# Copies moved behind exponentials and tails moved into the next softmax, in a one-core cross-attention kernel

## The chip, the cores and the metric

The kernel runs on one core of one Trainium2 chip. The metric is the device time of one execution in microseconds; for the kernel before it is the median of three runs. One more execution was profiled, and all lines quoted come from that one.

A core has five engines that run side by side, each with its own queue of instructions, in the order in which the program issues them. The profile calls them PE (matrix products, with PEld for its weight loads), DVE (VectorE), ACT (ScalarE), POOL (GpSimd) and SP (here it only issues DMAs). They wait for each other through semaphores.

## The reference

Layer norm, a query projection, attention over 32 heads of width 32 with keys and values taken straight from a context, an output projection, and the residual. Eight batches, 256 queries, 256 keys, width 1024, all float32.

```python
x = (hidden_states - mu) * rsqrt(var + LN_EPS) * ln_gamma + ln_beta
Q = split_heads(x @ Wq.T)
K = split_heads(memory_keys)                  # the same context for both
V = split_heads(memory_values)
scores = einsum('bhsd,bhtd->bhst', Q, K) * HEAD_DIM ** (-0.5)
scores = where(mask, scores, -inf)
probs = softmax(scores, axis=-1)
attn = einsum('bhst,bhtd->bhsd', probs, V)
out = attn.transpose(0, 2, 1, 3).reshape(B, S, HIDDEN) @ Wout.T
return residual + out
```

## The kernel before

**Quads.** The work is cut into 64 quads: four heads of one batch, eight quads to a batch (`N = 64`, `NQ = 8`). One loop over n walks through them as a software pipeline. Loop n issues, for PE in this order: the scores of quad n+1 (L471), some steps of an output product (L675), the values of quad n-2 (L605), more steps, a query projection (L332) or a query product (L432), and more steps. `softmax(n + 1)` is issued within the same loop, behind values n-2; it works on the scores just made, mostly on DVE, ACT and POOL.

**One softmax.** For each of the four heads j and both halves s of the queries, `exps(j)` issues a DVE pass that reads the scores in PSUM, adds the mask and finds a minimum (L505), and an ACT exponential that also sums (L509). `normalize(j)` is a DVE reciprocal (L516) and two POOL scalings (L518). `blocks(j)` transposes 32 by 32 blocks on DVE into the tile pT (L524). `aside(0)` and `aside(1)` copy half of pT for two heads each to the tile pc on ACT (L530). The last transpose `blocks(3)`, `aside(1)` and four DMAs on SP (pT to pT, L585, and pc to pT, L589), with the loop's loads and sends between them (`between`), form a function `tail`. After it pT has the layout that values need. For quads 0 to 7 the tail is put on a list `tails` and run within the next softmax, behind `exps(0)`; for all later quads it runs at once.

**Where the copies stand.** Behind `exps(0)` and the tails, `softmax_parts` copies finished values from PSUM to SBUF on ACT (`copy_at`, L618, two copies for a quad). The values have one pair of PSUM tiles, so the next values wait for these copies.

**Output products.** The output projection of a batch is done by seven products of 512 columns (`PRODUCTS`, four steps each, every step two matmul instructions in the profile), while the next batch's quads run. Their sums and differences of blocks are made on POOL (`sum_at`, L658). They accumulate in one PSUM bank (`ps_o`, one buffer). For batches 0 to 5 the first product, A11, is issued in loops n = 9, 17, 25, 33, 41 and 49 between scores and values; `keep_p1` (L683, ACT) then copies the bank, and the second product, A12, accumulates further into the same bank: three steps later in the same loop, the fourth in the next. `keep_p1` reaches the softmax as the hook "p1", run behind `exps(0)`. Later takes and stores from the bank are DVE instructions (L713, L717), hooked into later softmaxes. The same hooks mechanism isn't used for batch 6: its products (`ENDS`, one a loop, n = 56 to 62) run while the last batch's quads do, and their copies out of the bank (`keep_p1` at n = 57, `take_po_q`, L696, at n = 58, `copy_po`, L693, at n = 59 to 63) are issued ahead of the softmax of the loop. POOL adds them to the residual (`add_kept`, L701), SP sends them (L704). From n = 59 on, two matmul instructions a loop also go to the last batch's own output (L725).

**Query sums.** For batches 3 to 7 the query projection works on sums of blocks of the normalized input, made on POOL (`sum_x`, L422) from a tile that DMAs on SP fill (`move_x`, L319).

**Buffers.** e: 4; pT, pc: 3; scores: 4 PSUM banks, one for each head; values: one pair of tiles; `po`: one bank.

Of the kernel before, what the change touches and what calls it, by code (L numbers as in the profile page):

```python
# [59 lines left out]
def xattn_kernel(  # L60
# [16 lines left out]
    NQ = NC  # L77
# [9 lines left out]
    N = B * NQ  # L87
# [368 lines left out]
    mbs, scs, pTs, pvs, ats, pos = {}, {}, {}, {}, {}, {}  # L456
# [19 lines left out]
    def softmax(*args):  # L476
        for _ in softmax_parts(*args):
            pass

    tails = []  # L480

    def softmax_parts(n, copies=(), between=(), hooks={}, fill=()):

        fill = list(fill)

        def fill_in():
            if fill:  # L490
                fill.pop(0)()

        pss = scs[n]
        pT = pTs[n] = ptp.tile([P, 2, NI, NH, NS, K], F32, tag="pT", name=f"pT_{n}")
        pc = asp.tile([P, NI, NH, NS, K], F32, tag="pc", name=f"pc_{n}")
        es, mns, dens = {}, {}, {}

        def exps(j, part=range(NS)):
            if 0 in part:
                es[j] = ep.tile([P, NS, T], F32, tag="e", name=f"e_{n}_{j}")  # L500
                mns[j] = sm.tile([P, NS], F32, tag="mn", name=f"mn_{n}_{j}")
                dens[j] = sm.tile([P, NS], F32, tag="den", name=f"den_{n}_{j}")
            e, mn, den = es[j], mns[j], dens[j]
            for s in part:
                nc.vector.tensor_tensor_reduce(  # L505
                    out=e[:, s, :], in0=pss[j][:, s, :], in1=mbs[n // NQ], scale=1.0,
                    scalar=NO_SCORE, op0=ALU.add, op1=ALU.min, accum_out=mn[:, s : s + 1],
                )
                nc.scalar.activation(  # L509
                    e[:, s, :], e[:, s, :], AF.Exp, bias=mn[:, s : s + 1], scale=-1.0,  # L510
                    accum_out=den[:, s : s + 1],
                )

        def normalize(j):
            rden = sm.tile([P, NS], F32, tag="rden", name=f"rden_{n}_{j}")
            nc.vector.reciprocal(rden, dens[j])  # L516
            for s in range(NS):
                nc.gpsimd.tensor_scalar(  # L518
                    es[j][:, s, :], es[j][:, s, :], rden[:, s : s + 1], 1.0,
                    ALU.mult, ALU.mult,  # L520
                )

        def blocks(j):
            nc.vector.transpose(  # L524
                pT[:, :, :, j, :, :].rearrange("p a i s k -> p (a i) s k"),
                es[j].rearrange("p s (b t) -> p b s t", t=K),
            )

        def aside(j):
            nc.scalar.copy(pc[:, :, ts(j, 2)], pT[:, 1, :, ts(j, 2)])  # L530

        if n == 0:
            for j in range(NH - 1):
                exps(j, (0,))
            yield
            exps(NH - 1, (0,))
            fill_in()
            yield
            for j in range(NH):
                exps(j, (1,))  # L540
            normalize(0)
            fill_in()
        else:
            exps(0)
            for hook in hooks.get("p1", ()):
                hook()
            while tails:
                tails.pop()()
            for done in list(pvs):
                copy_at(done)  # L550
            exps(1)
            for hook in hooks.get("soon", ()):
                hook()
            exps(2)
            normalize(0)
            exps(3)
        if n <= NQ:
            for copy in copies:
                copy()
        for hook in hooks.get(0, ()):  # L560
            hook()
        normalize(1)
        fill_in()
        blocks(0)
        for hook in hooks.get(1, ()):
            hook()
        normalize(2)
        fill_in()
        blocks(1)
        aside(0)  # L570
        normalize(3)
        fill_in()
        blocks(2)
        while fill:
            fill_in()
        if n > NQ:
            for copy in copies:
                copy()

        def tail():  # L580
            blocks(3)
            aside(1)

            for r in range(2):
                nc.sync.dma_start(pT[ts(2 * r, K), 1], pT[ts(2 * r + 1, K), 0])  # L585
            for load in between:
                load()
            for r in range(2):
                nc.sync.dma_start(pT[ts(2 * r + 1, K), 0], pc[ts(2 * r, K)])  # L589

        if n < NQ:
            tails.append(tail)
        else:
            tail()
        yield
# [16 lines left out]
    def copy_at(n):  # L612
        b, c = divmod(n, NQ)
        k, c = divmod(c, NK)
        if c == 0:
            ats[b, k] = atp.tile([P, NK, NS, NA, K], F32, tag="at", name=f"at_{b}_{k}")
        for r, pv in enumerate(pvs.pop(n)):
            nc.scalar.copy(  # L618
                ats[b, k][:, c, :, ts(r, 2), :], pv.rearrange("p a s k -> p s a k")
            )  # L620
# [195 lines left out]
    early, late = (0, 1, 2, 3, 6, 7), (4, 5)  # L816
# [8 lines left out]
    for c in range(NC):  # L825
        copy_x0(1, c, nc.scalar if c < NC // 2 else nc.vector)
    first = softmax_parts(0, (partial(copy_q, 1),), (), {}, [
        partial(ln_stats, 1, 0), partial(ln_stats, 1, 1),
        partial(ln_norm, 1, 0, nc.vector), partial(ln_norm, 1, 1, nc.scalar),
# [14 lines left out]
    for b in range(B - 1):  # L844
        done, ends = 0, b == B - 2
        for i, counts in enumerate(ENDS if ends else STEPS):
            n = NQ * (b + 1) + i
# [16 lines left out]
    for n in range(N):  # L864
# [26 lines left out]
        hooks, now, behind = {}, [], []  # L891
# [136 lines left out]
```

## Time and profile before

| what | us |
|---|---|
| median of three runs | 590.96 (589.95 to 594.18) |
| the profiled execution | 589.45 |
| its span, first to last instruction | 587.7 |
| PE busy, of the span | 571.1 (97%) |
| DVE busy | 456.2 (78%) |
| ACT busy | 413.2 (70%) |
| POOL busy | 393.5 (67%) |

The granted clock of PE is 1.0 throughout. The page gives, for each group of instructions, its busy time and mean length, and the idle time of its engine just before it with what ended that idle time. Some of its groups:

| line, engine, what | count | mean ns |
|---|---|---|
| L505 DVE pass over scores | 512 | 415 |
| L509 ACT exponential | 512 | 501 |
| L518 POOL scaling | 512 | 478 |
| L524 DVE transpose | 256 | 708 |
| L530 ACT aside | 128 | 617 |
| L618 ACT copy of values | 128 | 254 |
| L675 PE product step (part in `po_S`) | 152 | 609 |

An instruction's printed length overlaps the next one's start on the same engine by a little, so the distance from start to start is what counts when instructions follow one another: eight L518 scalings in a row take 3.65 us at 308.49, less than eight times the mean. In timelines a row is: start, length, engine, line, operation, output and input tiles, shapes, count, and in brackets the idle time before it with its releaser. Rows that follow without a break are merged into one with a count.

### The profile page before, as it was taken

The numbers are of one execution on the slowest core, as the hardware profiler recorded it, in microseconds if no ns is written. First come the engines' busy times: TensorE is split into PE (matmuls) and PEld (weight loads), VectorE is DVE, ScalarE is ACT, GpSimd is POOL, SyncE is SP. The second block draws the span as 40 slices with busy tenths as digits, with TensorE's granted clock in tenths as the row PEclk, the third lists the DMA queues.
The fourth block names the chain that finished last, engine by engine and source line by source line (L and its number), as shares of the span: only waits on it lengthen the run. The fifth ranks groups of instructions, "written<-read, shape, count | busy, mean of one in ns | idle before, by whom it ended". The sixth has DMA issues, their size and how long they took to land.

```text
span 587.7 us, 19984 instructions
## 1 busy us (share of the span) xinstructions
PE 571.1 (97%) x7160; PEld 392.9 (67%) x7160; DVE 456.2 (78%) x1685; ACT 413.2 (70%) x1425; POOL 393.5 (67%) x662
## 2 busy tenths in 40 slices
PE   8999999999999999999999999999999999989997
PEld 8787785666667776677766776666776677644443
DVE  5878887888778799688878898688886778698701
ACT  4788886777668766696766976578776767578700
POOL 1568897899788895767549764587556674377700
PEclk9999999999999999999999999999999999999999
DMA  8566888656786778766886867956767866447451
GB/s 317 207 166 214 233 243 243 203 165 177 215 271 195 197 227 258 217 191 182 241 219 192 234 182 216 264 163 204 211 185 215 243 184 175 139 154 214 110 163 71
DMA packets 47907, 119.02 MB, mean 203 GB/s; under 512 B 9152, under 2 KB 9664, under 8 KB 47808
## 3 DMA queue, kind: packets, MB, share of 16 engines
q1 hardware_dynamic: 47520, 117.74, 68.1%
q8 instruction: 57, 0.93, 0.7%
q14 instruction: 42, 0.34, 0.2%
q10 hardware_dynamic: 288, 0.01, 0.0%
HBM read 66.33 MB, written 11.53 MB: 133 GB/s over the span
## 4 chain that ended last, share of the span: by engine, by line
PE 58%; POOL 17%; DVE 11%; issue 5%; ACT 3%; DMA 3%; SPq 1%; POOLq 0%; DVEq 0%; ACTq 0%
PE po_S L675 13%; POOL e L518 12%; PE pq_A L432 12%; PE sc L471 7%; PE pq L332 7%; PE pv L605 7%; PE po_A L675 6%; DVE e L505 5%; PE po L725 4%; DVE pT L524 3%; PE pq_S L432 2%; DVE st L225 2%; ACT e L509 1%; POOL sx L422 1%; DMA wq<-in_wq_dram 1%
## 5 line engine op out<-in xcount | busy, mean ns | idle before, releaser
L518 POOL TENSOR_SCALAR e<-e,rden 128x256 f32<-128x256 f32 x512 | 236.0, 478 | 98.0 <-DVE rden L516 94.4
L509 ACT ACTIVATE e<-e,mn 128x256 f32<-128x256 f32 x512 | 253.9, 501 | 34.2 <-DVE mn L505 34.1
L524 DVE STREAM_TRANSPOSE pT<-e 128x512 f32<-128x512 f32 x256 | 181.2, 708 | 49.8 <-POOL e L518 40.4
L505 DVE CUSTOM_DVE_ANT_0 e<-sc,mb 128x256 f32<-128x256 f32 x512 | 185.2, 415 | 16.2 <-PE sc L471 15.4
L530 ACT COPY pc<-pT 128x512 f32<-128x512 f32 x128 | 79.0, 617 | 85.3 <-DVE pT L524 52.8
L509 ACT ACTIVATION_READ_ACCUMULATOR e<-e,mn 128x1 f32 x512 | 98.0, 191 | 0.0
L332 PE MATMUL pq<-xnT,wq 128*128 128x256 f32 (+1 forms) x368 | 84.1, 382 | 1.3 <-ACT qa L339 1.2
L332 PEld LDWEIGHTS pq<-xnT,wq 128*128 128x128 f32 x368 | 68.7, 190 | 15.8 <-issue 3.3
L605 PE MATMUL pv<-pT,v 64*32 64x128 f32 x4096 | 74.4, 274 | 1.7 <-DMA pT<-pT 0.9
L675 PE MATMUL po_S<-wo,at 128*128 128x512 f32 x152 | 74.8, 609 | 1.3 <-ACT ends L693 0.6
L471 PEld LDWEIGHTS sc<-k,qa 32*128 32x128 f32 x1024 | 46.6, 184 | 43.2 <-issue 23.7
L605 PEld LDWEIGHTS pv<-pT,v 64*32 64x32 f32 x4096 | 57.3, 105 | 26.9 <-issue 14.2
L471 PE MATMUL sc<-k,qa 32*128 32x256 f32 x1024 | 74.8, 401 | 0.1
L675 PE MATMUL po_A<-wo,at 128*128 128x512 f32 x128 | 60.6, 609 | 3.2 <-ACT ends L693 2.8
L516 DVE RECIPROCAL rden<-den 128x2 f32<-128x2 f32 x256 | 38.3, 150 | 26.1 <-ACT e L509 23.9
L675 PE MATMUL po_S<-wo,s 128*128 128x512 f32 x104 | 50.2, 607 | 2.5 <-DVE r L717 1.8
L505 DVE DVE_READ_ACCUMULATOR2_ANT mn<- 128x1 f32 x512 | 42.5, 83 | 0.0
L675 PEld LDWEIGHTS po_A<-wo,at 128*128 128x128 f32 x128 | 22.6, 189 | 28.3 <-issue 22.3
L675 PEld LDWEIGHTS po_S<-wo,at 128*128 128x128 f32 x152 | 25.7, 190 | 22.3 <-issue 19.1
L432 PEld LDWEIGHTS pq_A<-xnT,wq 128*128 128x128 f32 x320 | 37.3, 192 | 4.8 <-issue 4.1
L432 PE MATMUL pq_A<-xnT,wq 128*128 128x128 f32 x320 | 37.3, 275 | 0.0
L618 ACT COPY at<-pv 128x128 f32<-128x128 f32 x128 | 26.2, 254 | 11.0 <-PE pv L605 11.0
(82 smaller groups left out, 589.4 us busy)
## 6 DMA issues: line engine op xcount, KB each, us to landing
v<-in_kv_dram SPq DMA_DIRECT2D x32, 512.0 KB
pT<-pT SPq DMA_DIRECT2D x128, 128.0 KB
pT<-pc SPq DMA_DIRECT2D x128, 128.0 KB
ring<-kept_T SPq DMA_DIRECT2D x18, 512.0 KB
k<-in_kv_dram SPq DMA_DIRECT2D x32, 256.0 KB
x<-in_x_dram SPq DMA_DIRECT2D x14, 512.0 KB
r<-in_x_dram SPq DMA_DIRECT2D x28, 256.0 KB
out_dram<-r SPq DMA_DIRECT2D x28, 256.0 KB
```

The costliest lines, as they stand in the source:

```text
L332: nc.tensor.matmul(pqs[n], wq[:, o, c, :], xnTs[b](c), start=(c == 0), stop=(c == NC - 1),)
L432: nc.tensor.matmul(pqs[b][:, o, :], w[:, c], x_[:, c], start=begins and o + c == 0, stop=c == NK - 1, skip_group_check=True,)
L471: nc.tensor.matmul(scs[n][j][:, s, :], qa[r, n % NQ, ts(s, P)], ks[n - n % 2][r, n % 2, :], start=True, stop=True,)
L505: nc.vector.tensor_tensor_reduce(out=e[:, s, :], in0=pss[j][:, s, :], in1=mbs[n // NQ], scale=1.0, scalar=NO_SCORE, op0=ALU.add, op1=ALU.m ...
L509: nc.scalar.activation(e[:, s, :], e[:, s, :], AF.Exp, bias=mn[:, s : s + 1], scale=-1.0, accum_out=den[:, s : s + 1],)
L516: nc.vector.reciprocal(rden, dens[j])
L518: nc.gpsimd.tensor_scalar(es[j][:, s, :], es[j][:, s, :], rden[:, s : s + 1], 1.0, ALU.mult, ALU.mult,)
L524: nc.vector.transpose(pT[:, :, :, j, :, :].rearrange("p a i s k -> p (a i) s k"), es[j].rearrange("p s (b t) -> p b s t", t=K),)
L530: nc.scalar.copy(pc[:, :, ts(j, 2)], pT[:, 1, :, ts(j, 2)])
L605: nc.tensor.matmul(pvs[n][r][j * HD : (j + 1) * HD], vs[n - n % 2][ts(r, 2 * K), i, ds(n % 2 * P + j * HD, HD)], pT[ts(r, 2 * K), :, i, j, ...
L618: nc.scalar.copy(ats[b, k][:, c, :, ts(r, 2), :], pv.rearrange("p a s k -> p s a k"))
L675: nc.tensor.matmul(po, operand(b, name)[:, c], wo[:, which, c], start=begins and c == 0, stop=c == NK - 1, skip_group_check=not begins,)
```

## The change

Two edits, both in `softmax_parts`.

- In a softmax that has the hook "p1" (quads 10, 18, 26, 34, 42 and 50), the hook `keep_p1` runs behind `exps(2)` and `normalize(0)`, ahead of `exps(3)`, instead of behind `exps(0)`. The copies of finished values, `copy_at`, run behind `exps(3)` in these softmaxes, instead of behind `exps(0)`. All other softmaxes keep their order.
- The tail of quads 57 to 62 is put on the list, as for quads 0 to 7, and runs within the next softmax behind `exps(0)`: last transpose, last aside, the four pT moves, and the loads and sends between them. Quads 8 to 56 and 63 keep their tail at once.

```diff
             exps(0)
-            for hook in hooks.get("p1", ()):
-                hook()
             while tails:
                 tails.pop()()
-            for done in list(pvs):
-                copy_at(done)
+            late = "p1" in hooks
+            if not late:
+                for done in list(pvs):
+                    copy_at(done)
             exps(1)
             for hook in hooks.get("soon", ()):
                 hook()
             exps(2)
             normalize(0)
+            for hook in hooks.get("p1", ()):
+                hook()
             exps(3)
+            if late:
+                for done in list(pvs):
+                    copy_at(done)
...
-        if n < NQ:
+        if n < NQ or N - NQ < n < N - 1:
             tails.append(tail)
         else:
             tail()
```

## The prediction

> **What bounds the kernel now.** I read the page's first part, then TensorE (PE) in order of time, then the two places of the change on ScalarE (ACT), VectorE (DVE) and GpSimd (POOL).
>
> ```profile
> span 587.7 us, 19984 instructions
> PE 571.1 (97%) x7160; PEld 392.9 (67%) x7160; DVE 456.2 (78%) x1685; ACT 413.2 (70%) x1425; POOL 393.5 (67%) x662
> ```
>
> PE holds the span, so the change is worth the PE waits that it removes or makes, and nothing else. I look at starts of matmuls and at the idle time printed before them. After quad 8 there is little. First the last batch, TensorE's rows in order of time (start, length, what, idle before and its releaser):
>
> ```profile
> 520.21 3.70 PE L675 MATMUL po_A<-wo,s 128*128 128x512 f32 x8 [0.55 <-POOL s L658]
> 528.20 3.70 PE L675 MATMUL po_A<-wo,at 128*128 128x512 f32 x8 [2.13 <-ACT ends L693]
> 535.56 3.70 PE L675 MATMUL po_A<-wo,at 128*128 128x512 f32 x8 [0.64 <-ACT ends L693]
> 543.02 3.67 PE L675 MATMUL po_S<-wo,s 128*128 128x512 f32 x8 [0.74 <-ACT ends L693]
> 550.30 3.70 PE L675 MATMUL po_S<-wo,at 128*128 128x512 f32 x8 [0.58 <-ACT ends L693]
> 557.83 1.31 PE L605 MATMUL pv<-pT,v 64*32 64x128 f32 x64 [0.83 <-ACT at L618]
> ```
>
> Six waits, 5.47 us. In four of them a product group waits until ScalarE has copied the group before out of the one `po` bank (copy_po, L693). ScalarE's rows there show why the copy is late:
>
> ```profile
> 532.44 0.62 ACT L530 COPY pc<-pT 128x512 f32<-128x512 f32 x1
> 534.41 0.62 ACT L530 COPY pc<-pT 128x512 f32<-128x512 f32 x1 [1.35 <-DVE pT L524]
> 534.93 0.58 ACT L693 COPY ends<-po_A 128x512 f32<-128x512 f32 x1
> ```
>
> The group was done when PE went on to the next work, 531.74. ScalarE was free at 532.97, but the copy stands behind the tail's aside (L530), which waits for the last transpose, which waits for POOL's last scaling: 1.35 us idle with a ready copy behind.
>
> Now the other place, the loop in which keep_p1 (L683) stands (n = 9, 17, 25, 33, 41, 49; here 33), ScalarE, then POOL:
>
> ```profile
> 303.18 0.49 ACT L509 ACTIVATE e<-e,mn 128x256 f32<-128x256 f32 x1
> ...
> 305.37 0.59 ACT L683 COPY p<-po_A 128x512 f32<-128x512 f32 x1 [1.61 <-PE po_A L675]
> 306.46 0.43 ACT L618 COPY at<-pv 128x128 f32<-128x128 f32 x2 [0.50 <-PE pv L605]
> 306.77 0.52 ACT L509 ACTIVATE e<-e,mn 128x256 f32<-128x256 f32 x1
> ```
> ```profile
> 307.25 1.26 POOL L422 TENSOR_TENSOR sx<-xnT 128x512 f32<-128x512 f32 x1 [4.93 <-DMA xnT<-xe]
> 308.49 3.65 POOL L518 TENSOR_SCALAR e<-e,rden 128x256 f32<-128x256 f32 x8
> ```
> ```profile
> 316.61 1.96 PE L675 MATMUL po_S<-wo,s 128*128 128x512 f32 x4 [0.63 <-DVE r L717]
> 386.62 1.95 PE L675 MATMUL po_S<-wo,s 128*128 128x512 f32 x4 [1.14 <-DVE r L717]
> ```
>
> ScalarE loses 306.77 - 303.67 = 3.1 us behind a product and then behind values, while six exponentials are ready. PE itself does not stop in this loop; the price shows one loop later, where a VectorE store comes late (0.63, 1.14 us). But POOL's scaling there also stands behind a query-side sum that waits for a DMA until 307.25.
>
> **What the Trainium skill says.** "Perfetto Trace Analysis", section Identifying the Most-Contended Engine: busy matmul time is a poor measure, because matmuls are pipelined, and weight loads are a better one. The trace agrees (97% beside 67%), hence the starts. "PSUM — Partial Sum Buffer", section Engine vs sequencer instructions: the queues of ScalarE, VectorE and GpSimd are strict FIFO. The three rows above show it. "Perfetto Trace Analysis", section Matmuls: independent groups should rotate through PSUM banks, so that one's evacuation overlaps the next one's matmuls. Here the groups share one bank, and the waits on L693 are that price; the change adds no bank, it can only bring the copy forward.
>
> **Part 1, keep_p1 and copy_at behind exponentials, six loops.** Nothing is added; two kinds of ScalarE copies change places. ScalarE: the exponentials of heads 1 and 2 come right behind those of head 0. For n = 33 six of them end at 303.18 + 0.50 + 4 x 0.49 = 305.64; the product ended before 305.37, so keep_p1 runs 305.64 to 306.23; head 3 to 307.2; copy_at to 307.6. So the last exponential moves from 309.74 to 307.2, 2.5 us.
> The new wait: product A12 needs the bank that keep_p1 reads, and stands on PE behind values. It begins at 306.35 today, set by values. keep_p1's end lies 0.12 us before it. The same sum for the others leaves 0.21 (n = 9), 1.85 (17, a query projection stands between), 0.15 (25), 0.23 (41), 0.27 (49). From a copy's end to the matmul that it frees the trace has 0.05 us (535.51 to 535.56), so this wait costs 0. If it is gone by 0.2 us each: five times 0.2 = 1.0 us. Queued behind A12 on PE are the next scores and values, whose other operands are ready.
> copy_at's late end (307.6): its readers are the next values' buffer, PE at 310.20, and the fourth A12 step, at 311.28; cover 2.6 us, cost 0.
> What it brings: only what POOL lets through. At n = 33, 41, 49 and 17 the eight scalings run without a gap behind that sum (x8, 3.65 us from 308.49), so an earlier exponential changes nothing: the waits 0.63 and 1.14 us stay, and so do two of 0.24 us in the loop after. At n = 25 a gap of 0.30 us inside the scalings closes, at n = 9 one of 0.77: the stalls behind these (start gaps of 0.19, 0.23 and 0.31 us on PE, at 256.40, 266.10 and 116.92) go. **Part 1: -0.7 us**; ends: +1.0 and -3.3 (if also 0.63 + 1.14 + 2 x 0.24 and the small start gaps around them go).
>
> **Part 2, tails of quads 57 to 62 inside the next softmax.** Per quad these move behind two passes of head 0: one transpose (DVE, L524, 0.71), one aside (ACT, L530, 0.53 from start to next start), four pT moves, and the loads and a send between them on SP. The same count; POOL gets nothing new.
> SP: a tail's issues span some 4 us (520.34 to 524.32), and SP idles 3.4 us before the next, so a shift of 1 to 3 us fits. The reader of pT is values, two loops on: from the last issue to it the trace has 554.79 - 546.51 = 8.3 us for quad 61, and 557.83 - 553.85 = 4.0 for quad 62, without a wait on DMA. "DMA: Bandwidth & Descriptors", section Anatomy of one DMA, gives about 2.0 us plus bytes over 436 GB/s (fitted on another issuing path): an estimate of 2.3 us for 128 KB; no landing is printed here. I keep 0.
> Forward through the loops, durations from the rows above, L505 passes at 0.345 us a step, exponentials 0.49, scalings 0.93 to 0.95 for two:
> (a) n = 57. DVE is idle here until scores come (512.80), so the transpose of quad 57, done today in idle time, now delays passes 3 to 6 and the reciprocal by 0.69: scaling starts 515.8 instead of 515.13, S2's sum ends 520.85 instead of 520.15, PE waits 1.25 us in place of 0.55. **+0.7**.
> (b) n = 59. ScalarE, after exponentials (525.3) and the first aside (526.1), copies at once, to 526.65; PE's values end at 526.7. The wait of 2.13 us goes, margin 0.05.
> (c) n = 60, 61, 62. The copy ends 0.25, 0.35 and 0.6 us before values do. 0.64 + 0.74 + 0.58 go. The loop falls from 7.36 us (528.20 to 535.56) to PE's own 3.54 + 0.95 + 1.08 + 1.09 = 6.7; ScalarE then needs about 6.0 (eight exponentials 3.93, two asides, copy_at, copy_po), DVE about 6.2, POOL 5.1 to 6.3. PE is next in line. (b) and (c): **-4.1**.
> (d) n = 63. Its own tail stays immediate, and copy_po and copy_at of quad 61 still stand behind it. From scores 63 on PE to values 62 today: 547.48 to 557.83, 10.35 us, a chain of softmax 63. Tail 62 now sits inside it, but the place where copy_po held ScalarE (exponentials began 1.1 us after the first pass) is gone; they about cancel (10.3 to 10.5). PE comes earlier, so its wait grows from 0.83 to about 1.45: **+0.6**.
> From there to the end all shifts alike. Part 2: -4.1 + 0.7 + 0.6 = **-2.8 us**. Ends: 0 (if the bank's copy comes late by some other wait) and -4.1.
>
> **Sum**: -3.5 us on the profiled execution, 589.45 (span 587.7, and 1.75 around it) to 585.95. That execution lies 1.5 us under the median of the runs shown, 590.96, so for the median I say 590.96 - 3.5 = 587.5.
>
> **Rivals.**
> A, more comes through: the sum behind the DMA is not what holds softmax 34 and 42, all of part 1's 3.3 us come: 590.96 - 3.3 - 2.8 = 584.9. For it: ScalarE's 3.1 us hole is before every one of these stalls. Against it: the unbroken x8 behind 308.49.
> B, part 2 gives nothing: the margins in (b) and (c), 0.05 to 0.6 us, are too thin, or S2's delay carries on; then 590.3, or with part 1 at 0, 591. For it: the thin margins. Against it: every loop's PE work is 0.65 us shorter than its period, and two waits would have to fail at once.
> C, slower: keep_p1 behind six exponentials makes A12 wait, at all five places with thin cover. At 1.5 us each (head 2's passes held up, or a copy that waits its turn behind another): 5 x 1.5 - 0.25 x 5 cover, about +6.2, less part 2's 2.8: 594.4. It decides once A12 waits more than 0.7 us at each place (3.5 / 5). Against it: DVE's six passes end at 304.08, well ahead of the exponentials.
> That the change doesn't do what it says: the tails list could be empty where it is popped; the loop pops it in each later softmax, so I see no way.
>
> **How the numbers follow.** A measurement here tells about 1%, 5.9 us, from no change: faster is under 585.05, slower over 596.87. My forecast (585.5 to 589) 0.62, rival A (583.5 to 585.5) 0.13, rival B (589 to 591.3) 0.16, rival C (above 591.3) 0.09. Over 1% faster: most of A and a little of the forecast's low end with a quiet set of runs, 0.12; over 1% slower: the far half of C, 0.05; else 0.83. The range leaves out the low half of A and C: 584.6 to 591.0.
>
> **What would show it.** Right: no idle before L675 with releaser L693 after quad 58, product groups 6.7 us apart; one larger POOL wait (about 1.2 us) before the S2 group; a larger ACT wait (about 1.5) before values 62; keep_p1 behind six exponentials, A12 at values' end; the 0.63 and 1.14 us waits on L717 still there. Wrong: any wait on L683 before A12, waits on pT moves before L605, or groups still 7.3 us apart. The whole would be wrong if PE's matmuls themselves ran at another pace.

## The result, and the profile after

| | before | changed |
|---|---|---|
| median of ten runs | 591.53 us (589.47 to 596.35) | 586.95 us (585.12 to 589.42) |
| span of the profiled execution | 587.7 us | 583.3 us |

The ratio is 0.9908, 95% interval 0.9882 to 0.9934: 0.92% faster (0.66 to 1.18%), 5.4 us of 591.53 (3.9 to 7.0). The two medians of the table lie 4.6 us (0.77%) apart, within that interval. The forecast was 587.5, a gain of 3.5; the size is a little short, and it is the last batch that gave more.

First part of the page, changed kernel:

```profile
span 583.3 us, 19985 instructions
PE 570.0 (98%) x7160; PEld 392.6 (67%) x7160; DVE 453.4 (78%) x1685; ACT 412.2 (71%) x1425; POOL 393.0 (67%) x662
```

TensorE (PE) is still the bound, and its work is the same: 7160 matmuls. Only its waits can have changed. Its rows in the last batch, in order of time (start, length, engine and line, operation, tiles, count, idle before with its releaser); lines of the softmax's parts stand one further down than before (L509 is now L510), those below them six (L675 is now L681):

```profile
519.97 3.70 PE L681 MATMUL po_A<-wo,s 128*128 128x512 f32 x8 [0.97 <-POOL s L664]
...
525.83 3.70 PE L681 MATMUL po_A<-wo,at 128*128 128x512 f32 x8
...
532.48 3.70 PE L681 MATMUL po_A<-wo,at 128*128 128x512 f32 x8
...
539.13 3.70 PE L681 MATMUL po_S<-wo,s 128*128 128x512 f32 x8
...
545.78 3.70 PE L681 MATMUL po_S<-wo,at 128*128 128x512 f32 x8
...
553.52 1.31 PE L611 MATMUL pv<-pT,v 64*32 64x128 f32 x64 [1.04 <-ACT at L624]
```

The four waits on `copy_po` are gone, with no other in their place; the groups follow each other after 6.65 us (525.83, 532.48, 539.13, 545.78) in place of 7.28 to 7.46. The waits ahead of the first group and of values 62 grew, to 0.97 and 1.04. ScalarE (ACT) shows why the copy comes in time:

```profile
530.84 0.62 ACT L531 COPY pc<-pT 128x512 f32<-128x512 f32 x1
531.36 0.58 ACT L699 COPY ends<-po_A 128x512 f32<-128x512 f32 x1
532.14 0.51 ACT L510 ACTIVATE e<-e,mn 128x256 f32<-128x256 f32 x1 [0.19 <-DVE mn L506]
...
533.14 0.60 ACT L531 COPY pc<-pT 128x512 f32<-128x512 f32 x1
```

What stands ahead of the copy of the bank (L699) is now the first aside of the quad, whose transposes are done; the second aside comes two exponentials later, at 533.14, and by then waits for nothing. The copy ends at 531.94; PE goes from values to the next group at 532.48.

Now the other place, the loop of n = 33, ScalarE:

```profile
305.56 0.49 ACT L510 ACTIVATE e<-e,mn 128x256 f32<-128x256 f32 x1
306.05 0.56 ACT L689 COPY p<-po_A 128x512 f32<-128x512 f32 x1
306.51 0.51 ACT L510 ACTIVATE e<-e,mn 128x256 f32<-128x256 f32 x1
307.02 0.49 ACT L510 ACTIVATE e<-e,mn 128x256 f32<-128x256 f32 x1
307.51 0.40 ACT L624 COPY at<-pv 128x128 f32<-128x128 f32 x2
```

and the three engines behind it, PE, then GpSimd (POOL), then VectorE (DVE):

```profile
306.87 2.84 PE L681 MATMUL po_A<-wo,at 128*128 128x512 f32 x6
...
316.70 1.96 PE L681 MATMUL po_S<-wo,s 128*128 128x512 f32 x4 [0.20 <-DVE r L723]
```
```profile
307.34 1.26 POOL L422 TENSOR_TENSOR sx<-xnT 128x512 f32<-128x512 f32 x1 [4.60 <-DMA pT<-pT]
308.58 3.65 POOL L519 TENSOR_SCALAR e<-e,rden 128x256 f32<-128x256 f32 x8
```
```profile
309.54 0.71 DVE L525 STREAM_TRANSPOSE pT<-e 128x512 f32<-128x512 f32 x1 [4.13 <-POOL e L519]
```

ScalarE's hole of 3.1 us is closed: all exponentials are done by 307.5. `keep_p1` ends at 306.61 and product A12 starts behind values at 306.87, without a wait. Yet POOL does not scale earlier. It idles 4.60 us ahead of the query sum (L422), which waits for a DMA, with the scalings queued behind it, and DVE idles 4.13 us for POOL. (The releaser is inferred; the sum reads the tile that `move_x` fills.)

**Where the time went.** All kernels here issue the same 7160 matmuls in the same order, so the start of each can be set against its twin, the same matmul in the kernel before. The table gives, worked out from the traces, how many us longer (+) or shorter (-) than before PE takes for three stretches of the kernel before: behind the loop n = 9 (110.87 to 127.54 us), behind n = 25 (254.43 to 267.91), and the last batch (513.51 to 562.61):

| kernel | ratio to before, 95% | n = 9 | n = 25 | last batch |
|---|---|---|---|---|
| changed | 0.9908 (0.9882 to 0.9934) | -0.41 | +0.03 | -3.56 |
| after_again | 0.9923 (0.9897 to 0.9949) | -0.41 | -0.62 | -3.56 |
| p1_only | 1.000 (0.998 to 1.0021) | -0.42 | +0.88 | -0.01 |
| p2_only | 0.9935 (0.9916 to 0.9953) | 0.00 | +0.82 | -3.64 |
| p2_from58 | 0.9926 (0.9904 to 0.9948) | -0.41 | -0.63 | -3.44 |
| tail63_late | 0.992 (0.9892 to 0.9948) | -0.41 | -0.09 | -3.64 |
| keep_behind_eight | 0.9954 (0.9935 to 0.9973) | -0.41 | -0.54 | -3.61 |
| s1_late_before | 0.9959 (0.9942 to 0.9977) | -0.02 | +0.06 | -0.01 |
| s1_late_after | 0.9856 (0.9819 to 0.9894) | -0.41 | -0.62 | -3.60 |
| p2_s1_late | 0.9872 (0.9847 to 0.9897) | +0.01 | -0.07 | -3.63 |
| all_three | 0.984 (0.9807 to 0.9873) | -0.42 | -0.62 | -4.05 |
| loads_early | 0.9829 (0.9803 to 0.9855) | -0.42 | -0.63 | -3.97 |

The experiments in it are told below. Of the 4.4 us between the two profiled spans, 3.56 lie in the last batch and 0.41 at n = 9; the rest is drift between executions: by 513 us the starts stand +3.6 to -0.8 us from their twins in the kernels whose query sum stays where it was. It is not the clock: `p1_only`, with the +3.6, was granted 1.0 like the kernel before.

The expectations quoted below forecast the span of one profile, and with this drift such a span can't decide between forecasts 1 to 3 us apart. (The spans: `p1_only` 591.2 us, `p2_only` 586.4, `after_again` 583.7, `s1_late_before` 587.4, `s1_late_after` 580.2, `p2_s1_late` 582.9, `keep_behind_eight` 586.7, `p2_from58` 585.1, `tail63_late` 584.5, `all_three` 580.0, `loads_early` 580.6.) So each is judged by the wait that it names, by the twins and by the timed ratio, not by its span.

### The profile page after: what moved, and what is told of

Same layout as the page of the kernel before. It is cut to its first block, busy times and chain, and to the rows that moved or that the text cites. A ratio compares the mean times of both kernels' runs of the same rounds, so it can differ in the third digit from the quotient of the medians.

```text
span 583.3 us, 19985 instructions
## 1 busy us (share of the span) xinstructions
PE 570.0 (98%) x7160; PEld 392.6 (67%) x7160; DVE 453.4 (78%) x1685; ACT 412.2 (71%) x1425; POOL 393.0 (67%) x662
## 4 chain that ended last, share of the span: by engine, by line
PE 60%; POOL 14%; DVE 10%; DMA 7%; issue 4%; ACT 2%; SPq 2%; POOLq 0%; DVEq 0%; ACTq 0%
PE po_S L681 14%; PE pq_A L432 10%; POOL e L519 10%; PE pq L332 8%; PE sc L471 7%; PE pv L611 7%; PE po_A L681 6%; DVE e L506 4%; PE po L731 4%; DVE pT L525 3%; PE pq_S L432 2%; DMA wq<-in_wq_dram 2%; POOL sx L422 2%; DMA x<-in_x_dram 1%; DMA pT<-pT 1%
## 5 line engine op out<-in xcount | busy, mean ns | idle before, releaser
L510 ACT ACTIVATE e<-e,mn 128x256 f32<-128x256 f32 x512 | 253.9, 500 | 38.6 <-DVE mn L506 38.5
L510 ACT ACTIVATION_READ_ACCUMULATOR e<-e,mn 128x1 f32 x512 | 97.7, 191 | 0.0
L681 PE MATMUL po_S<-wo,at 128*128 128x512 f32 x152 | 74.6, 608 | 0.9 <-DVE r L719 0.9
L681 PE MATMUL po_A<-wo,at 128*128 128x512 f32 x128 | 60.6, 608 | 0.4 <-ACT qa L341 0.4
L681 PE MATMUL po_S<-wo,s 128*128 128x512 f32 x104 | 50.2, 607 | 0.5 <-DVE r L723 0.5
L432 PEld LDWEIGHTS pq_A<-xnT,wq 128*128 128x128 f32 x320 | 37.3, 192 | 4.8 <-issue 3.8
L681 PEld LDWEIGHTS po_S<-wo,at 128*128 128x128 f32 x152 | 25.8, 190 | 21.2 <-issue 19.3
L681 PEld LDWEIGHTS po_A<-wo,at 128*128 128x128 f32 x128 | 22.6, 189 | 25.4 <-issue 21.4
L432 PE MATMUL pq_A<-xnT,wq 128*128 128x128 f32 x320 | 37.3, 275 | 0.0
L714 POOL TENSOR_TENSOR r<-r,p 128x512 f32<-128x512 f32 x18 | 23.1, 1284 | 14.1 <-DMA r<-in_x_dram 14.1
```

Source lines behind the costliest of these rows:

```text
L432: nc.tensor.matmul(pqs[b][:, o, :], w[:, c], x_[:, c], start=begins and o + c == 0, stop=c == NK - 1, skip_group_check=True,)
L510: nc.scalar.activation(e[:, s, :], e[:, s, :], AF.Exp, bias=mn[:, s : s + 1], scale=-1.0, accum_out=den[:, s : s + 1],)
L681: nc.tensor.matmul(po, operand(b, name)[:, c], wo[:, which, c], start=begins and c == 0, stop=c == NK - 1, skip_group_check=not begins,)
```

## The experiments

**Each part alone.** `p1_only` is the changed kernel without part 2, `p2_only` the kernel before with part 2 alone.

```diff
 p1_only, against the changed kernel
-        if n < NQ or N - NQ < n < N - 1:
+        if n < NQ:
 p2_only, against the kernel before
-        if n < NQ:
+        if n < NQ or N - NQ < n < N - 1:
```

> Part 1 alone, all tails after quad 7 at once. Theory (part 1 is gated by POOL's sum behind the DMA): span about 587.0, 0.7 us under before; in loop 33 and 41 the scalings still run unbroken behind L422, and from 500 us on all waits of the kernel before are there (2.1, 0.6, 0.7, 0.6 us on the po copies). Rival A (the hole in ScalarE was the cause): span about 584.4, 3.3 us less. Rival (what the first 500 us gained was a difference in DMA times between two executions): span within 0.3 us of 587.7.

> Part 2 alone, keep_p1 and copy_at as before. Theory: span about 584.1 (3.6 us less than before), the product groups of the last batch 6.65 us apart, no wait on the po copies after quad 58, the S2 wait at about 1.0 us. Rival (the two parts need each other, ScalarE must be early from quad 50 on): part 2 alone gives 2 us or less, span 585.7 or more.

`p1_only` has the waits on `copy_po` as before, `p2_only` has none (last batch, PE's rows):

```profile
531.79 3.70 PE L681 MATMUL po_A<-wo,at 128*128 128x512 f32 x8 [2.13 <-ACT ends L699]
```
```profile
523.09 3.70 PE L675 MATMUL po_A<-wo,s 128*128 128x512 f32 x8 [1.06 <-POOL s L658]
...
556.58 1.31 PE L605 MATMUL pv<-pT,v 64*32 64x128 f32 x64 [1.03 <-ACT at L618]
```

Part 2 alone is 0.65% faster (0.47 to 0.84), 3.8 us of 592.23, and its trace gives 3.64 of them in the last batch; its span, 2.4 us of drift later at 513 us, would have spoken for the rival. Part 1 alone can't be told from no change: -1.2 to +1.2 us. Its span is above all that was expected of it, by the drift of 3.6 us. What it does in softmax 34 is seen in POOL's row and in the PE row that this leads to:

```profile
310.29 1.26 POOL L422 TENSOR_TENSOR sx<-xnT 128x512 f32<-128x512 f32 x1 [5.40 <-DMA pT<-pT]
```
```profile
319.66 1.95 PE L681 MATMUL po_S<-wo,s 128*128 128x512 f32 x4 [1.01 <-DVE r L723]
```

From the start of the sum to the matmul that waits for the store it is 319.66 - 310.29 = 9.37 us. Before it was 316.61 - 307.25 = 9.36, in the changed kernel 316.70 - 307.34 = 9.36, in `p2_only` 318.47 - 309.10 = 9.37. So with or without part 1 the sum's start sets the store.

**The changed kernel once more**, unaltered, to see what one execution is worth.

> The changed kernel once more, unaltered. Theory (the waits before the S2 group's store in loops 34 and 42 follow the landing of the input's DMAs, not the change): the last batch gains the same 3.6 us as in the first profile, while the two waits near 317 and 386 us, 0.20 and 0.26 in the first profile, may come out anywhere from 0.2 to 2 us, and the span from 583 to 586. Rival (part 1 made those waits small): both stay below 0.4 us.

```profile
315.37 1.96 PE L681 MATMUL po_S<-wo,s 128*128 128x512 f32 x4 [0.86 <-DVE r L723]
...
385.80 1.96 PE L681 MATMUL po_S<-wo,s 128*128 128x512 f32 x4 [1.57 <-DVE r L723]
```

The same program now waits 0.86 and 1.57 us where the first profile had 0.20 and 0.26. The sum started at 306.01, again 9.36 us ahead of the matmul at 315.37. That these waits had shrunk in the first profile of the changed kernel was therefore no work of the change. The last batch repeats to 0.01 us (-3.56 twice), and the ratio agrees.

**The query sum moved.** If the sum that waits for a DMA holds softmax 34 and 42, it must help to put it behind the scalings, and if ScalarE's hole matters once POOL is free, part 1 must then pay. The sum S1 of the loop is taken out of the list ahead of the softmax and issued behind it, in the kernel before, in the changed one, and in `p2_only`:

```diff
 s1_late_before, s1_late_after, p2_s1_late
             softmax(n + 1, copies, between, hooks, fill)
+            if n + 1 in firsts:
+                sum_x(firsts[n + 1], "S1")
...
-        for slot, name in ((n + 2, "S1"), (n + 1, "S2"), (n + 1, "S4"), (n - 1, "S3")):
+        for slot, name in ((n + 1, "S2"), (n + 1, "S4"), (n - 1, "S3")):
```

> The kernel before, with only the query sum S1 moved behind the next softmax's scalings. Theory: with POOL free, ScalarE's hole of 3.1 us behind keep_p1 becomes what holds the scalings; they wait for exponentials, and the softmax ends some 0.5 us earlier than before at the most: span 586.9 to 587.7, so that part 1 is then worth 2 us or more (the difference of the two moved-sum kernels, after part 2's 3.6 is taken off). Rival (the DMA wait alone was the cause, ScalarE's hole never mattered): span about 585.5, as much gain as with part 1.

> The changed kernel, and the query sum S1 (L422, which waits for a DMA) is issued on POOL behind the scalings of the next softmax instead of ahead of them. Theory: in the loops of part 1 the scalings begin with their own exponentials, VectorE's hole of 4.1 us before the first transpose in loop 33 goes, and the four waits of 0.2 to 0.3 us on takes and stores one and two loops later go: span about 582.0, 1.3 us under the changed kernel. Rival (S1 then comes late for its product): waits before L432 instead, span 583.3 or more.

> Part 2 and the moved sum S1, without part 1. The difference to the changed kernel with S1 moved (span 580.2, 1.44% under before) is part 1 alone, with the varying DMA wait out of the way. Theory now (part 1 is worth what it saves at n = 9, 0.4 us, and small gaps at 33 and 41): span 580.8 to 581.5, ratio to before 0.986 to 0.988. Rival (ScalarE's hole matters once POOL is free): span 583 or more, ratio 0.990 or more.

`s1_late_before`, ScalarE, POOL and PE in loop 33:

```profile
304.94 0.49 ACT L509 ACTIVATE e<-e,mn 128x256 f32<-128x256 f32 x1
307.24 0.59 ACT L683 COPY p<-po_A 128x512 f32<-128x512 f32 x1 [1.72 <-PE po_A L675]
```
```profile
306.10 0.93 POOL L518 TENSOR_SCALAR e<-e,rden 128x256 f32<-128x256 f32 x2 [2.02 <-DVE rden L516]
310.04 2.89 POOL L518 TENSOR_SCALAR e<-e,rden 128x256 f32<-128x256 f32 x6 [3.01 <-DVE rden L516]
312.90 1.26 POOL L422 TENSOR_TENSOR sx<-xnT 128x512 f32<-128x512 f32 x1
```
```profile
314.21 3.84 PE L432 MATMUL pq_S<-sx,ring 128*128 128x128 f32 x32
317.89 1.88 PE L675 MATMUL po_S<-wo,s 128*128 128x512 f32 x4
```

ScalarE's hole is still there (POOL idles 3.01 us for it between the second and the third scaling), and the waits on the store are gone all the same. The sum's own product (L432) does not wait for it either. So my theory in that run, in which this hole would go on to hold these places, fell, though the span lay where it said; the rival, that the sum held them, stands.

From 299.57 to 403.04 us of the kernel before, PE is shorter by 2.68 us in `s1_late_before` and by 2.67 in `p2_s1_late`, which have no part 1, and by 2.89, 3.21 and 3.27 in `all_three`, `s1_late_after` and `loads_early`, which have it: with the sum out of the way 0.2 to 0.6 us are left for part 1 there. In the kernels whose sum stays, the same stretch came out anywhere from 1.32 us shorter to 1.79 us longer, with a wait on the store of 0.20 to 1.83 us in all of them near 317 us, so the exact 2.7 belongs to the one profile of the kernel before. Timed, `s1_late_before` is 0.41% faster than before (0.23 to 0.58), 2.4 us. `s1_late_after` is 1.44% faster, more than I expected, since I had counted only the waits that the first profile of the changed kernel happened to show.

`p2_s1_late` is `s1_late_after` without part 1: 0.9872 against 0.9856, a ratio as the theory had it (the span, 582.9, lies between theory and rival), with intervals that overlap widely. Its trace lacks the -0.41 at n = 9 and the -0.62 at n = 25.

**The thin cover at keep_p1.** The prediction left 0.12 to 0.27 us between the end of `keep_p1` and the start of A12 at five places. One more pair of exponentials, 1.0 us, tests whether that was read rightly:

```diff
 keep_behind_eight, against the changed kernel
             normalize(0)
+            exps(3)
             for hook in hooks.get("p1", ()):
                 hook()
-            exps(3)
```

> The changed kernel, but keep_p1 stands behind all eight exponentials instead of six. Theory: A12 on PE waits for it at the five places with thin cover, 0.98 us later less 0.1 to 0.3 us cover, some 0.8 us each; one place (n = 17) has 1.85 us cover and stays. Most of it adds up, save where PE waits anyway one loop later: span 583.3 + 2.5 to 4.0. Rival (the cover is larger than the trace shows, or PE's later waits swallow it): span within 1 us of 583.3.

ScalarE's copy, PE's row behind it, and the line of the view of waits (engine, line, releaser: us in total, times, longest):

```profile
307.71 0.56 ACT L689 COPY p<-po_A 128x512 f32<-128x512 f32 x1
```
```profile
308.32 2.84 PE L681 MATMUL po_A<-wo,at 128*128 128x512 f32 x6 [0.71 <-ACT p L689]
```
```profile
PE po_A L681 <- ACT p L689: 3.6, 5, 0.8
```

Five waits, 3.6 us in all: 1.0 us later costs 0.7 to 0.8 at each place with thin cover (0.23 to 0.29 us in the changed kernel), and nothing at n = 17 (1.78 us there). Timed, the gain falls to 0.46%, from 0.92 and 0.77 in the two measurements of the changed kernel; against the second the intervals still overlap.

**The rest of the last batch.** Two waits had grown. `p2_from58` leaves the tail of quad 57 at once, to take back the wait ahead of the first group; `tail63_late` also puts off the tail of quad 63, which then no longer stands ahead of the copies that values 62 wait for; `all_three` is both, with the sum moved; `loads_early` also issues the loop's loads ahead of the tail, so that they no longer stand between the moves.

```diff
 p2_from58, against the changed kernel
-        if n < NQ or N - NQ < n < N - 1:
+        if n < NQ or N - NQ + 1 < n < N - 1:
 tail63_late, against the changed kernel
-        if n < NQ or N - NQ < n < N - 1:
+        if n < NQ or N - NQ < n < N:
...
             copy_at(n - 2)
+            while tails:
+                tails.pop()()
 all_three: s1_late_after and tail63_late, and
+        if n < NQ or N - NQ + 1 < n < N:
 loads_early: all_three, and
+            if n >= NQ:
+                for load in between:
+                    load()
+                between = ()
             tails.append(tail)
```

> The changed kernel, but quad 57 keeps its tail at once (58 to 62 are moved). Theory: the tail of 57 is the one that costs, since it leaves idle VectorE time and delays S2's sum; the wait before the S2 group falls from 0.97 back to about 0.5 us and the span from 583.3 to about 582.8. Rival (the late sum has another cause, the rest of POOL's queue): the wait stays at 1.0 and the span at 583.3.

> The changed kernel, and quad 63's tail is moved too, behind the last copy out of the po bank and the copy of values 61. Theory: the wait of 1.04 us before values 62 goes, because these two copies no longer stand behind the last aside; values 63 keep their cover (today 3 us or more from the last pT move), span about 582.3. Rival (the end is set by values 63, whose pT moves come later): the wait moves to values 63 and the span stays within 0.3 us of 583.3.

> The changed kernel with the three further moves together: quad 57's tail at once, quad 63's tail behind the last two copies, S1 behind the next scalings. Theory: the three gains lie in different loops and add up, 0.5 + 1.0 + 1.3: span about 580.5, and about 1.8% under the kernel before in the timed runs. Rival (one of them only shifts a wait): 581.5 or more.

> The kernel with the three further moves, and the loads and sends of the moved tails are issued at once, at the end of their own softmax, instead of between the pT moves of the next. Theory: values 62 wait for the last pT move of quad 62, which stands on SP and in the DMA queues behind a load of 512 KB; with that load some 4 us earlier the waits of 0.52 and 0.41 us there go, span about 579.2. Rival (the moves land late for another reason, the traffic as such): the wait on pT moves stays at 0.5 us or more, span 580 or more.

PE's rows with a wait in the last batch, `p2_from58`, then `tail63_late`, then `all_three`, then `loads_early`:

```profile
521.07 3.70 PE L681 MATMUL po_A<-wo,s 128*128 128x512 f32 x8 [0.55 <-POOL s L664]
...
555.01 1.55 PE L611 MATMUL pv<-pT,v 64*32 64x128 f32 x64 [1.49 <-DMA pT<-pc]
```
```profile
554.42 1.58 PE L611 MATMUL pv<-pT,v 64*32 64x128 f32 x64 [0.73 <-DMA pT<-pc]
```
```profile
549.61 0.38 PE L611 MATMUL pv<-pT,v 64*32 64x128 f32 x2 [0.52 <-DMA pT<-pc]
...
550.40 1.13 PE L611 MATMUL pv<-pT,v 64*32 64x128 f32 x62 [0.41 <-DMA pT<-pc]
```
```profile
550.33 0.38 PE L615 MATMUL pv<-pT,v 64*32 64x128 f32 x2 [0.73 <-DMA pT<-pc]
```

In `p2_from58` the first wait falls back to 0.55, and values 62 wait 0.45 us longer: the last batch gains nothing by it (-3.44). There the moves of quad 62's pT come last, in the changed kernel the copies. SP issues their second pair at 551.76 us; the changed kernel does so at 549.29, or at 550.33 on a stretch as late as this one (values 61 start 1.04 us later). The load issued just ahead takes SP 1.70 us in place of 0.57; why is not settled.

`tail63_late` takes the copies out of the way and meets the moves, 0.73 us, at the same values, which neither its theory nor its rival had; gained: 0.08. Both edits together give 0.4 to 0.5 us (-4.05, -3.97), where 1.5 was expected of them; that the span of `all_three` came out as forecast is owed to the sum, which gave more, and to drift.

The wait on the moves stays. With the load ahead of the tail it is 0.73 us and then 0.29, in place of 0.52 and 0.41, so the theory of `loads_early` fell. The load now stands ahead of the first pair instead: the last of this pair lands at 548.23, 3.63 us after its issue. SP's issues of quad 62's moves in `loads_early` (start and length of the issuing):

```profile
544.05 1.29 SPq L591 DMA_DIRECT2D pT<-pT  x2
547.94 1.14 SPq L595 DMA_DIRECT2D pT<-pc  x2
```

The second pair starts 547.94 - 544.05 - 1.29 = 2.60 us after the first was issued. It writes the part of pT that the first pair reads, and the trace gives the first pair's landing as what SP waited for; it then lands 2.25 and 2.36 us after its own issues. So two landings follow one another. That this order is what remains there is argued from these rows; no kernel with another order, or without the load, was run.

`all_three` and `loads_early` are the fastest measured, 1.6% (1.27 to 1.93) and 1.71% (1.45 to 1.97) under the kernel before; the two can't be told apart, nor from `s1_late_after`.

## Why the prediction was right or wrong

**What bounds the kernel**: right. PE's work did not change, and the gains that could be placed are waits of PE's that went. (That 97% stands beside 67% shows only that the two measures differ, not which is the better one.)

**Part 1, cost 0**: right. A12 starts at the end of values in the changed kernel, no wait on `keep_p1` anywhere; the cover is 0.23 to 0.29 us where 0.12 to 0.27 was read, and `keep_behind_eight` shows that it is no thicker. Rival C, slower by such waits, was a matter of 1 us of ScalarE's time.

**Part 1, gain 0.7**: right in its mechanism. The scalings of softmax 34 and 42 stand behind the sum that waits for a DMA; eight scalings still run unbroken behind it (3.65 us from 308.58), and the store follows its start by 9.36 us with part 1 or without. The gain at n = 9, where no query sum is issued, is 0.41 in all eight profiles that have part 1 unaltered, and in `keep_behind_eight`; it is absent in the three without. (I had 0.31.) At n = 25 it is 0.54 to 0.63 in six of those nine (I had 0.42); in the other three, the first profile of the changed kernel among them, it does not show. There PE waits for a late take from the bank (L719 in the changed kernel), 0.25 to 0.72 us each; the four profiles without part 1 all have such a wait, 0.07 to 0.67. Why it comes in three of the nine is open. So part 1 is worth 0.4 to 1.0 us; timed alone its interval holds both, and 0. Rival A, all 3.3 us of it, falls. The step "the waits 0.63 and 1.14 stay" held for its reason, but not as numbers: they are 0.20 and 0.26 in one execution of the changed kernel, 0.86 and 1.57 in the other.

**Part 2, (b) and (c), -4.1**: right, all four waits went, at 6.65 us from group to group where 6.7 was said. By the starts of the groups it is -2.13, -0.71, -0.81 and -0.63, together -4.28: a start follows its wait by a little more than the idle time printed. The thinnest margin, said to be 0.05, measured 0.20: the copy of n = 59 ends at 525.63, the group starts at 525.83. Rival B falls with it.

**Part 2, (a), +0.7**: mis-sized, +0.51 measured by the group's start (519.97 for 520.21, on a stretch that runs 0.75 us earlier than before). The scalings do start late by what was said (514.98 for 515.13, so 0.60). But they then run eight in 3.71 us, where before it took 3.79, so less of the delay reaches the sum.

**Part 2, (d), +0.6**: mis-sized, +0.21 measured (1.04 for 0.83). From scores 63 to values 62 the chain takes 553.52 - 543.62 = 9.90 us, where I kept 10.3 to 10.5. VectorE's rows show the term that I left out, in the kernel before and then in the changed one:

```profile
548.39 0.71 DVE L524 STREAM_TRANSPOSE pT<-e 128x512 f32<-128x512 f32 x1 [0.27 <-POOL e L518]
549.03 0.39 DVE L505 CUSTOM_DVE_ANT_0 e<-sc,mb 128x256 f32<-128x256 f32 x1
```
```profile
544.78 0.42 DVE L506 CUSTOM_DVE_ANT_0 e<-sc,mb 128x256 f32<-128x256 f32 x1 [0.22 <-PE sc L471]
...
545.48 0.71 DVE L525 STREAM_TRANSPOSE pT<-e 128x512 f32<-128x512 f32 x1
```

Before, the last transpose of quad 62 stands ahead of the first pass over scores 63, which begins 549.03 - 547.48 = 1.55 us after these scores start on PE. In the changed kernel it stands behind two passes, and the first begins 544.78 - 543.62 = 1.16 us after. I had counted the tail as work that comes into this chain, and not that its transpose leaves the chain's head. From the first pass to values 62 it is 8.80 us before and 8.74 after, so the rest cancels as I had it. As measured, the sum of part 2 is -4.28 + 0.51 + 0.21 = -3.56 where I had -2.8. The profiled execution came out 0.8 us under its sum, 585.12 for 585.95. That the two differences agree is chance: part 1 gave less there than I had said (0.41 at n = 9, nothing at n = 25), and drift made up for it.

**SP and the DMAs at 0**: right as a cost, with luck. The moves of quad 62 were said to have a spare of 4.0 us from the last issue. In the changed kernel that issue is at 550.07 and lands at 553.32, 0.20 us before values 62 start, and these wait for a copy; in `p2_from58` the moves come last. "DMA: Bandwidth & Descriptors" of the Trainium skill, section Anatomy of one DMA, had given an estimate of 2.3 us for 128 KB, from a fit on another issuing path. Two lines of the changed kernel's page, DMA issues with the median from issue to landing, agree for one pair of moves and not for the other:

```profile
pT<-pT SPq DMA_DIRECT2D x128, 128.0 KB, 2.5
pT<-pc SPq DMA_DIRECT2D x128, 128.0 KB, 5.1
```

The landings that the traces record, one by one, tell the pairs apart. In the changed kernel the second pair takes a median of 3.8, 5.0 and 6.4 us where one, two or three other transfers were issued between the two pairs (7, 31 and 23 landings); in `loads_early` nine landings with none between take 2.22 to 2.55 us. So the estimate is met where no load stands between, and missed behind loads.

**The total**: 3.5 said, 3.9 to 7.0 timed in the first measurement, and 0.77% (0.51 to 1.03), 3.0 to 6.1 us, in the second. The traces account for 3.56 and for 0.4 to 1.0, together 4.0 to 4.6 us. That 587.5 lies as near to 586.95 as it does is partly luck: the three runs that I started from had a median of 590.96, the ten runs 591.53, so about half of what the gain was short by (3.5 for 4.6 between medians) is hidden in the start.

## What to carry to other kernels

A copy that is ready but queued behind a waiting instruction can hold up its consumer; putting the waiting instruction behind work that is ready removed four PE waits here at once, 4.1 us (3.6 net). Before an engine's order is improved, ask what stands ahead on the next engine of the chain: ScalarE's 3.1 us hole was worth nothing in softmax 34 while GpSimd's scalings stood behind a sum that waited for a DMA, and moving that one sum alone gave 2.4 us (1.4 to 3.4). Where a bound engine issues the same instructions in both kernels, set the starts of twins against each other stretch by stretch, and run the same program twice before a change in a wait behind a DMA is called an effect: here two such waits changed by 0.7 and 1.3 us without any edit.

## What the runs showed of the hardware

- A move of 128 KB between tiles on the chip lands 2.22 to 2.55 us after its issue when no load was issued between it and the pair of moves ahead (nine landings in `loads_early`), and after a median of 3.8, 5.0 and 6.4 us with one, two or three transfers of other tiles between (changed kernel).
- The last batch repeats to 0.01 us between two executions of one program, while at 300 us the same two stand 2.0 us apart, and two waits there that follow the landing of a DMA change from 0.20 to 0.86 and from 0.26 to 1.57 us.
